# Four graph layers on one core: a new hand-set plan for VectorE's order, and gathers released in batches of four

## The chip, the core and the metric

The kernel runs on one core of one Trainium2 chip. The core has five engines that run side by side, each working off its own list of instructions in order: TensorE (PE, with its weight loads shown as PEld), VectorE (DVE), ScalarE (ACT), GpSimd (POOL) and SyncE (SP, which here only starts transfers). The metric is the time of one execution on the device in microseconds (us), the median of several executions; lower is better.

## What is computed

There are 16 graphs of 1024 nodes with 64 features each and a dense 1024 x 1024 weighted adjacency matrix per graph, of which only a few entries in a row are not zero. Four layers follow each other, each with a layer norm and a ReLU ahead and a residual sum behind:

```python
h = relu(layernorm(x)); x = x + (tanh(concat(h, adj @ h) @ W1 + b1) @ W2 + b2)     # layer 0
h = relu(layernorm(x)); x = x + ((adj + I) @ h) / rowsum(adj + I)                  # layer 1
h = relu(layernorm(x)); x = x + mlp(h + agg(h, dilate(adj)))                       # layer 2
h = relu(layernorm(x)); x = x + ((adj @ h) / colsum(adj)) @ Wn + h @ Ws + bias     # layer 3
```

In layer 2, `dilate` takes some neighbours out of each node's list, and `agg` is a weighted sum of the 0.25, 0.5 and 0.75 quantiles, feature by feature, over the neighbours that are left. That is a sort of a short, ragged list of 64-wide rows for every node, and it is where most of the work lies.

## The kernel before

**Nodes in order of their number of neighbours.** For each graph the kernel ranks the 1024 nodes by their count of remaining neighbours and cuts the ranking into eight blocks of 128 nodes, one node on each of the 128 partitions. A block needs room for as many neighbours as its largest node has; `PLACES = [21, 19, 17, 16, 15, 13, 12, 11]` is how many neighbours of a block are fetched by gathers. `GROUPS` puts the blocks in five groups: block 0 alone (38 places, the longest lists being filled in by packed rows), block 1 alone, and then three pairs of blocks (2,3), (4,5), (6,7), which are sorted two at a time side by side.

**Six streams and a planner.** The work of a graph is cut into six Python generators: `adjacency` (loads the adjacency, transposes it, finds the neighbours to drop, ranks the nodes), `layers` (layers 0 and 1 and the norm of layer 2), `tail` (the rest of layer 2, layer 3 and the output), `gathers`, `neighbour_lists` (finds for each node the indices of its neighbours, eight at a time with MAX8) and `sorts` (the sorting network and the weighted sums). The streams run on different graphs at the same time. The order in which their instructions are put into each engine's list is fixed when the program is built, by a small planner at the end of `direct_path`. It keeps an imagined clock for each engine (`clk.dve`, `clk.pe`, `clk.act`, `clk.pool`). A stream adds its estimated costs to these clocks and then yields the imagined time at which its next result will be there, its due time. The planner takes the first stream, in the order in which they are named above, whose due time is not after `clk.dve`; if there is none, it moves `clk.dve` on to the earliest due time. The helper `after(dve, pe, act, lat)` computes a due time: the work of each engine behind that of the one before, and `lat` on top. Nothing of this clock exists on the chip. There every engine takes its list in order and waits at an instruction whose input is not there yet, with all that stands behind it.

**Gathers and their gate.** A gather is an indirect DMA that GpSimd starts: it fetches one row of 64 features for each of 128 nodes from the table `h_d` in DRAM into the tile `raw` (line 1274, 124 of them in a graph). GpSimd also starts the loads of the key rows that `neighbour_lists` searches (line 1086, eight in a graph, tile `k`), the packed rows (line 1255, three in a graph) and the return gather of the sums, `res` (line 1346, eight in a graph). The gate (lines 912 to 918) ties GpSimd to VectorE: VectorE writes a one-element mark, and GpSimd copies it, so that GpSimd does not go past this point before VectorE has come to the mark in its own list. A gate is set at most once in 4.0 us of the imagined VectorE clock. In `gathers` it is asked for at every fourth place `s`; for a pair of blocks that is every eight gathers.

**Lines that the prediction's steps touch.** 846 to 856 `preln`, the layer norm, with two due times; 940 and 962 the start and the end of the first half of `adjacency`; 998 and 1003 the marks of the dropped neighbours, one for each of eight blocks; 1038 and 1040 two tiles `spread` that VectorE writes and TensorE multiplies with ones, both in one buffer of the tag `ab`; 1045 the eight ACT passes that count for the ranking and 1048 VectorE's `pos` made of them; 1101, 1110 to 1117 the rounds of MAX8, one round of three instructions for each eight neighbours after the first eight; 1192 and 846 the handover from layer 0 to the next norm (`stat<-pt`); 1217 the first VectorE instruction that reads the sums of layer 1 (`den`); 1360 the first that reads the perceptron of layer 2 (`mid`); 1395 the first that reads layer 3; 1307 the compare-exchange steps of the sorting network; 1326 the weighted sums.

Of the kernel before, what the change touches and what calls it, by code (L numbers as in the profile page):

```python
# [11 lines left out]
U16 = mybir.dt.uint16  # L12
# [43 lines left out]
PLACES = [21, 19, 17, 16, 15, 13, 12, 11]  # L56
PACKS, NPACK = [(0, 0, 21, 2, 64), (1, 0, 23, 1, 32), (1, 32, 24, 4, 24), (2, 0, 28, 10, 12)], 3
KB = 4

# [670 lines left out]
def direct_path(ctx: ExitStack, tc: tile.TileContext, t: dict, out: bass.AP, flag):  # L730
# [70 lines left out]
    nc.gpsimd.dma_start(mask8, nodemask.rearrange("b (i p) -> (b i) p", p=P))  # L801
    maskf = lists.tile([B * NB, P], F32, tag="ab", name="maskf", bufs=1)
    nc.vector.tensor_copy(maskf, mask8)
# [37 lines left out]
    def preln(u, x, ha):  # L841

        s = nodes.tile([P, 4, NB], F32, name="stat")
        xc = mid(u, [P, NB, C])
        sq = mid(u, [P, NB, C])
        nc.vector.tensor_reduce(s[:, 0], x, AX.X, ALU.add)
        ts(s[:, 1], s[:, 0], 1.0 / C, None, op0=ALU.mult)
        tt(xc, x, s[:, 1, :, None].to_broadcast([P, NB, C]), ALU.subtract)
        act(sq, xc, AF.Square)
        yield after(1.5, act=0.65)  # L850
        nc.vector.tensor_reduce(s[:, 2], sq, AX.X, ALU.add)
        act(s[:, 3], s[:, 2], AF.Sqrt, bias=eps, scale=1.0 / C)
        yield after(0.7, act=1.0)
        nc.vector.reciprocal(s[:, 2], s[:, 3])
# [57 lines left out]
    def gate():  # L912
        if not marks or clk.dve > marks[-1] + 4.0:
            k = len(marks)
            nc.vector.memset(slots[:, k % 8:k % 8 + 1], 0.0)  # L915
            clk.dve += 0.15
            nc.gpsimd.tensor_copy(opened[:, k % 2:k % 2 + 1], slots[:, k % 8:k % 8 + 1])  # L917
            marks.append(clk.dve)
# [14 lines left out]
    def adjacency(b):  # L933
# [26 lines left out]
        sf = nodes.tile([P, 4, NB], F32, name="sf")  # L960
        yield clk.act + 0.3
        tt(mn[:, 2], mn[:, 0], mn[:, 1], ALU.add)
# [20 lines left out]
        for i in range(NB):  # L983
            following = flipped(i + 1) if i + 1 < NB else None

            p = bank2()
            for j in range(NB):
                o, e = j * P, (j // 4 + 1) * 512
                nc.tensor.matmul(p[:, o:e], nbt[:, j, :], stair[:, :e - o], start=j % 4 == 0, stop=j % 4 == 3)  # L989

            for q in range(2):
                s = slice(q * 512, (q + 1) * 512)
                act(gone[:, i, s], p[:, s], AF.Abs, bias=sf[:, 2 + q, i:i + 1], scale=2.0)  # L993
            nbt = following
            ready = after(0, pe=3.7, act=2.4)
            if waiting:
                yield waiting[1]
                ts(gone[:, waiting[0], :], gone[:, waiting[0], :], sf[:, 1, waiting[0]:waiting[0] + 1], -1.0,
                   op0=ALU.is_equal, op1=ALU.mult)
                clk.dve += 0.5  # L1000
            waiting = (i, ready)
# [34 lines left out]
        for q in range(2):  # L1036
            spread = lists.tile([P, 4, P], F32, tag="ab", name="spread", bufs=1)
            tt(spread, identf[:, None, :].to_broadcast([P, 4, P]),
               key[:, 4 * q:4 * q + 4, None].to_broadcast([P, 4, P]), ALU.mult)
            nc.tensor.matmul(p[:, q * 512:(q + 1) * 512], onesf, spread.rearrange("p j m -> p (j m)"),  # L1040
                             start=True, stop=True)
        over = nodes.tile([P, NB], F32, name="over")
        for i in range(NB):
            sink = lists.tile([P, N], F16, tag="ab", name="sink", bufs=1)
# [9 lines left out]
        nc.vector.tensor_copy(ph, pi)  # L1054
        low = lists.tile([P, NB, P], F16, tag="ab", name="low", bufs=1)
        tt(low, pidx[:, None, :].to_broadcast([P, NB, P]), ph[:, 0, :, None].to_broadcast([P, NB, P]), ALU.is_equal)
# [20 lines left out]
    def neighbour_lists(b):  # L1077
# [5 lines left out]
        def load_keys(i):  # L1083
            if i < NB:
# [12 lines left out]
        for b0, n, cap, *_ in GROUPS:  # L1097
            for i in range(b0, b0 + n):
                src, at = ks[i]
                yield at  # L1100
                nc.vector.max(out=found[:, o:o + 8], in_=src)  # L1101
                clk.dve += 1.15
                yield clk.dve
                less, before = src.bitcast(I16), None
                for r in range(1, -(-cap // 8)):


                    least = found[:, o + 7:o + 8]
                    if r == 1:
                        ts(less, src, least, None, op0=ALU.subtract)  # L1110
                    else:
                        ts(less, less, before, least, op0=ALU.add, op1=ALU.subtract)
                    before = least
                    most = nodes.tile([P, 8], U16, name="most")
                    nc.vector.max(out=most, in_=less.bitcast(U16))  # L1115
                    o += 8
                    ts(found[:, o:o + 8], most.bitcast(I16), 0.0, least, op0=ALU.min, op1=ALU.add)
                    clk.dve += 1.8
                    yield clk.dve
                o += 8  # L1120
                load_keys(i + KB)
        index = lists.tile([P, total], I32, name="index")
# [51 lines left out]
    def layers(b):  # L1174
# [17 lines left out]
        nc.scalar.copy(x, p)  # L1192
        yield after(0, pe=1.3, act=2.1) + 2.8
        ha = nodes.tile([P, NB, C + 1], F32, name="ha")
# [18 lines left out]
        done.add(("adjt", b))  # L1213
        yield after(0, pe=10.5, act=1.1) + 2.5
        clk.act += 10
# [21 lines left out]
    def gathers(b):  # L1237
        g = state[b]
        yield max(g["rows_at"], clk.pool)
        for k, (b0, n, cap, *_) in enumerate(GROUPS):  # L1240
            while not (b == 0 or ("sort", b - 1, k) in done):
                yield None
            raw = raws.tile([P, cap, n * C], F32, name=f"raw{k}")
            o = sum(c * -(-r // 8) * 8 for _, c, r, *_ in GROUPS[:k])
            clk.pool = max(clk.pool, clk.dve)
# [6 lines left out]
            if k == 0:  # L1252
                packed = nodes.tile([P, NPACK * C], F32, name="packed", bufs=1)
                for l, size in enumerate(sizes):
                    nc.gpsimd.indirect_dma_start(packed[:size, l * C:(l + 1) * C], None, h_ds[b % 3],
                                                 bass.IndirectOffsetOnAxis(ap=g["pack"][:size, l:l + 1], axis=0))
                    clk.pool += 1.27
                rows_d = dram.tile([NPACK, P, C], F32, name="rows_d")
            for s in range(cap):
                if s % 4 == 0:  # L1260
                    gate()
# [7 lines left out]
                for i in range(n):  # L1269
                    if s >= PLACES[b0 + i]:  # L1270
                        continue
                    clk.pool += 1.27
                    at = o + i * -(-cap // 8) * 8 + s
                    nc.gpsimd.indirect_dma_start(raw[:, s, i * C:(i + 1) * C], None, h_ds[b % 3],  # L1274
                                                 bass.IndirectOffsetOnAxis(ap=g["index"][:, at:at + 1], axis=0))
                if s % 4 == 3:
                    yield clk.pool - 5
# [62 lines left out]
    def tail(b):  # L1340
# [51 lines left out]
        zn = per_node(bank(), mt, w3n, 4)  # L1392
        yield after(0, pe=2.6)
        o = mid(1, [P, NB, C])
# [16 lines left out]
    programs = [_program(*group[2:]) for group in GROUPS]  # L1411
    edge = lists.tile([1, 2, C], F32, tag="ab", name="edge", bufs=1)
    nc.vector.memset(edge[:, 0], 0.0)
# [165 lines left out]
```

## Time and profile before

| | before |
|---|---|
| median of 3 executions | 4034.94 us (4027.11 to 4052.91) |
| span of the profiled execution | 4035.0 us |
| TensorE busy | 2059.4 us, 51% |
| VectorE busy | 3070.5 us, 76% |
| ScalarE busy | 1426.3 us, 35% |
| GpSimd busy | 2592.2 us, 64% |
| mean granted TensorE clock | 0.676 |

The profile counts an engine as busy while one of its instructions runs. On GpSimd a gather is busy only while its transfer is being set up; the short gap to the next one is listed as idle time that "issue" ended. The views used below are the page itself, the groups of instructions by line (a row has the line, engine and operation, the tiles, the count, the busy time, the mean of one in ns, and the idle time ahead of them with what ended it), the list of waits (who waited, for whom, us in total, times, longest), the timeline (start, length, engine, line, and in brackets the idle time ahead), and the busy time by stage.

### The profile page before, as it was taken

The numbers are of one execution on the slowest core, as the hardware profiler recorded it, in microseconds if no ns is written. First come the engines' busy times: TensorE is split into PE (matmuls) and PEld (weight loads), VectorE is DVE, ScalarE is ACT, GpSimd is POOL, SyncE is SP. The second block draws the span as 40 slices with busy tenths as digits, with TensorE's granted clock in tenths as the row PEclk, the third lists the DMA queues.
The fourth block names the chain that finished last, engine by engine and source line by source line (L and its number), as shares of the span: only waits on it lengthen the run. The fifth ranks groups of instructions, "written<-read, shape, count | busy, mean of one in ns | idle before, by whom it ended". The sixth has DMA issues, their size and how long they took to land.

```text
span 4035.0 us, 32061 instructions
## 1 busy us (share of the span) xinstructions
PE 2059.4 (51%) x8483; PEld 1008.6 (25%) x8483; DVE 3070.5 (76%) x7173; ACT 1426.3 (35%) x2658; POOL 2592.2 (64%) x2608
## 2 busy tenths in 40 slices
PE   7543745446464556456555564544655465544033
PEld 3312322222322223132322223222232222212011
DVE  2647877788687979868776888957969786996973
ACT  6523434333444334244343434323344343331000
POOL 1166666667576768747666676846857666775772
PEclk9665757767666677666667675666667667766555
DMA  2314133232524333242332424323252332323111
GB/s 96 114 40 123 48 115 93 86 107 53 163 50 143 76 107 98 57 134 62 124 84 78 115 65 128 79 76 105 51 164 53 125 88 86 84 62 111 44 47 57
DMA packets 237344, 362.40 MB, mean 90 GB/s; under 512 B 126848, under 2 KB 128496, under 8 KB 237152
## 3 DMA queue, kind: packets, MB, share of 16 engines
q1 hardware_dynamic: 156912, 255.00, 18.4%
q0 software_dynamic: 80096, 104.70, 12.8%
q8 instruction: 69, 1.13, 0.1%
q14 instruction: 123, 1.01, 0.1%
q10 hardware_dynamic: 144, 0.56, 0.0%
HBM read 245.26 MB, written 114.81 MB: 89 GB/s over the span
## 4 chain that ended last, share of the span: by engine, by line
DVE 51%; PE 13%; another core or an unknown queue 12%; issue 10%; ACT 6%; DMA 4%; POOL 4%; DVEq 0%; SPq 0%; ACTq 0%; POOLq 0%
DVE other L1307 14%; DVE raw L1307 14%; PE pt L875 6%; DVE most L1115 4%; POOL raw L1274 4%; DVE agg L1326 2%; DVE found L1101 2%; ACT adjt L1210 2%; PE pt L899 1%; DMA adjt_d<-adjt 1%; DVE nb L940 1%; ACT nb L954 1%; DVE k L1110 1%; DMA raw<-h_d,index 1%
## 5 line engine op out<-in xcount | busy, mean ns | idle before, releaser
L1274 POOL DMA_INDIRECT raw<-h_d,index x1984 | 2164.2, 1091 | 575.4 <-issue 548.5
L875 PE MATMUL pt<-adjt,ha 128*65 128x512 f32 (+1 forms) x1024 | 491.7, 642 | 169.4 <-DVE ha L1197 92.2
L1307 DVE TENSOR_TENSOR other<-raw 128x512 f32<-128x512 f32 (+11 forms) x816 | 536.1, 688 | 43.9 <-DMA raw<-h_d,index 27.3
L917 POOL COPY gate<-mark 1x1 f32<-1x1 f32 x293 | 96.6, 330 | 477.8 <-DVE mark L915 457.6
L947 PE MATMUL pt<-ef,a 128*128 128x128 f32 x1024 | 222.1, 388 | 299.9 <-ACT adjt L948 168.5
L1307 DVE TENSOR_TENSOR raw<-other 128x512 f32<-128x512 f32 (+10 forms) x464 | 356.4, 792 | 6.5 <-DVE other L1307 1.1
L989 PE MATMUL pt<-eh,nbt 128*128 128x512 f16 (+3 forms) x1024 | 207.1, 358 | 225.5 <-ACT nbt L978 152.0
L1115 DVE MAX8 most<-k 128x8 uint16<-128x1024 uint16 x224 | 275.1, 1228 | 15.4 <-DVE k L1110 4.1
L875 PEld LDWEIGHTS pt<-adjt,ha 128*65 128x65 f32 (+1 forms) x1024 | 149.2, 149 | 491.9 <-issue 432.0
L947 PEld LDWEIGHTS pt<-ef,a 128*128 128x128 f32 x1024 | 181.5, 206 | 336.5 <-ACT adjt L948 192.9
L1086 POOL DMA_INDIRECT k<-keys_d,node x128 | 131.4, 1026 | 208.8 <-DVE node L1071 112.9
L1022 ACT ACTIVATE nb<-pt 128x1024 f16<-128x1024 f32 x128 | 130.5, 1020 | 355.1 <-PE pt L1018 113.6
L876 ACT COPY big<-pt 64x1024 f32<-64x1024 f32 (+1 forms) x32 | 32.2, 1007 | 559.6 <-PE pt L875 300.0
L948 ACT COPY adjt<-pt 128x512 f32<-128x512 f32 x256 | 138.9, 583 | 242.1 <-PE pt L947 80.6
L1307 DVE TENSOR_TENSOR raw<-other,raw 128x640 f32<-128x640 f32 (+3 forms) x448 | 216.9, 495 | 7.7 <-remote 1.9
L1307 DVE TENSOR_TENSOR raw<-raw,other 128x128 f32<-128x128 f32 (+7 forms) x496 | 212.4, 437 | 12.2 <-remote 4.4
L1307 DVE TENSOR_TENSOR other<-other,raw 128x128 f32<-128x128 f32 (+4 forms) x448 | 201.8, 461 | 8.2 <-remote 2.3
L954 ACT ACTIVATE nb<-nb 128x512 f16<-128x512 f16 x256 | 159.7, 630 | 135.1 <-DVE nb L942 68.6
L993 ACT ACTIVATE gone<-pt,sf 128x512 f16<-128x512 f32 x256 | 162.8, 691 | 112.2 <-remote 46.5
L1018 PE MATMUL pt<-eh,gone 128*128 128x128 f16 x1024 | 132.7, 261 | 124.5 <-DVE gone L1003 37.8
L989 PEld LDWEIGHTS <-nbt 128*128 128x128 f16 x1024 | 102.9, 114 | 321.0 <-ACT nbt L978 164.3
L978 ACT COPY nbt<-pt 128x1024 f16<-128x1024 f16 x128 | 128.5, 1015 | 146.6 <-remote 106.4
(182 smaller groups left out, 4402.1 us busy)
## 6 DMA issues: line engine op xcount, KB each, us to landing
a<-in_adj_dram SPq DMA_DIRECT2D x64, 1024.0 KB
adjt_d<-adjt SPq DMA_DIRECT2D x64, 1024.0 KB
at<-adjt_d SPq DMA_DIRECT2D x128, 512.0 KB
keys_d<-nb SPq DMA_DIRECT2D x64, 512.0 KB
raw<-h_d,index POOLq DMA_INDIRECT x1984
x<-in_x_dram SPq DMA_DIRECT2D x16, 256.0 KB
h_d<-h SPq DMA_DIRECT2D x16, 256.0 KB
agg_d<-agg SPq DMA_DIRECT2D x16, 256.0 KB
```

The lines of the kernel that those rows point to most:

```text
L875: nc.tensor.matmul(p[p0:p0 + n, s], h[:, j, :n], adjt[:, j, s], start=j == 0, stop=j == NB - 1)
L947: nc.tensor.transpose(p[:, u * P:(u + 1) * P], a[:, j * P:(j + 1) * P], identf)
L948: nc.scalar.copy(adjt[:, 4 * q:4 * q + 4, i * P:(i + 1) * P], p.rearrange("p (u m) -> p u m", m=P))
L954: act(nb[:, i, s], nb[:, i, s], AF.Copy, accum_out=mn[:, q, i:i + 1])
L989: nc.tensor.matmul(p[:, o:e], nbt[:, j, :], stair[:, :e - o], start=j % 4 == 0, stop=j % 4 == 3)
L993: act(gone[:, i, s], p[:, s], AF.Abs, bias=sf[:, 2 + q, i:i + 1], scale=2.0)
L1018: nc.tensor.matmul(p[:, d], gone[:, j, i * P:(i + 1) * P], big_i, start=False, stop=j == 4 * q + 3 and i // 4 != q)
L1022: act(nb[:, i, :], p, AF.Relu)
L1086: nc.gpsimd.indirect_dma_start(k, None, g["keys_d"], bass.IndirectOffsetOnAxis(ap=g["node"][:, i:i + 1], axis=0))
L1115: nc.vector.max(out=most, in_=less.bitcast(U16))
L1274: nc.gpsimd.indirect_dma_start(raw[:, s, i * C:(i + 1) * C], None, h_ds[b % 3], bass.IndirectOffsetOnAxis(ap=g["index"][:, at:at + 1], axi ...
L1307: tt(view(two[to], *((i, vi) if greater else (j, vj)), w), view(two[s], i, vi, w), view(two[u], j, vj, w), ALU.max if greater else ALU.min)
```

## The change

The instructions stay nearly the same; what changes is mainly where the planner puts them.

- Due times are set later: in `preln`, at the end of the first half of `adjacency`, in its two loops, ahead of `key`, `pos` and `node`, after each of the two layers in `layers`, and at four places of `tail`. The planner is to hold VectorE's reading instruction back until the result is there, and to put other work ahead of it. Some TensorE costs in the plan grow for the same reason.
- A gather costs 1.39 us in the plan instead of 1.27.
- The gates: asked for after every four gathers in the pairs too, the least distance of two gates is 3.0 us instead of 4.0, and there is one more ahead of a graph's first key rows.
- The tiles of the tag `ab` get the pool's two buffers instead of one.
- The lengths of the neighbour lists come from a table by block, `LISTS`. Block 3 has 16 places to fetch and now finds 16 neighbours instead of 24, so one round of MAX8 less in each graph.

```diff
+LISTS = [40, 24, 24, 16, 16, 16, 16, 16]
...
-        yield after(1.5, act=0.65)
+        yield after(1.5, act=0.65, lat=1.2)
...
-        yield after(0.7, act=1.0)
+        yield after(0.7, act=1.0, lat=1.5)
...
-        clk.pe = max(clk.pe, clk.dve) + 1.5
+        clk.pe = max(clk.pe, clk.dve) + 2.0 * len(hs)
...
-        if not marks or clk.dve > marks[-1] + 4.0:
+        if not marks or clk.dve > marks[-1] + 3.0:
...
-        yield clk.act + 0.3
+        yield clk.act + 4.0
         tt(mn[:, 2], mn[:, 0], mn[:, 1], ALU.add)
...
-            ready = after(0, pe=3.7, act=2.4)
+            ready = after(0, pe=3.7, act=2.4, lat=3.0)
...
-        yield clk.act + 0.3
+        yield clk.act + 2.0
         key = nodes.tile([P, NB], F32, name="key")
...
-            spread = lists.tile([P, 4, P], F32, tag="ab", name="spread", bufs=1)
+            spread = lists.tile([P, 4, P], F32, tag="ab", name="spread")
...
-        yield after(1.6, pe=1.3, act=10.5)
+        yield after(1.6, pe=1.3, act=10.5, lat=2.0)
...
-        yield after(2.3, pe=1.2, act=0.2) - 0.2
+        yield after(2.3, pe=1.2, act=0.2) + 1.5
...
+        gate()
         for i in range(KB):
             load_keys(i)
-        total = sum(n * -(-cap // 8) * 8 for _, n, cap, *_ in GROUPS)
+        total = sum(LISTS)
...
-                for r in range(1, -(-cap // 8)):
+            for r in range(1, LISTS[i] // 8):
...
-        yield after(0, pe=1.3, act=2.1) + 2.8
+        yield after(0, pe=3.4, act=2.1) + 7.0
...
-        yield after(0, pe=10.5, act=1.1) + 2.5
+        yield after(0, pe=14.0, act=1.1) + 6.0
...
-                    clk.pool += 1.27
+                    clk.pool += 1.39
...
-                if s % 4 == 0:
+                if s % (4 // n) == 0:
                     gate()
...
-                if s % 4 == 3:
+                if (s + 1) % (4 // n) == 0:
                     yield clk.pool - 5
...
-        yield after(0, pe=2.2, act=1.5) + 3.2
+        yield after(0, pe=6.5, act=2.1) + 6.0
         o = mid(1, [P, NB, C])
...
-        yield after(0, pe=3, act=0.6, lat=0.5)
+        yield after(0, pe=3.5, act=0.6, lat=3.0)
...
-        yield after(0, pe=2.6)
+        yield after(0, pe=2.6, lat=5.0)
```

More of the change, by code (lines that the diff above doesn't have):

```diff
@@ L801, in direct_path @@
     nc.gpsimd.dma_start(mask8, nodemask.rearrange("b (i p) -> (b i) p", p=P))
-    maskf = lists.tile([B * NB, P], F32, tag="ab", name="maskf", bufs=1)
+    maskf = lists.tile([B * NB, P], F32, tag="ab", name="maskf")
     nc.vector.tensor_copy(maskf, mask8)
@@ L1043, in adjacency @@
         for i in range(NB):
-            sink = lists.tile([P, N], F16, tag="ab", name="sink", bufs=1)
+            sink = lists.tile([P, N], F16, tag="ab", name="sink")
             act(sink, p, AF.Sign, bias=neg[:, i:i + 1], accum_out=over[:, i:i + 1])
-        yield after(1.6, pe=1.3, act=10.5)
+        yield after(1.6, pe=1.3, act=10.5, lat=2.0)
         pos = nodes.tile([P, NB], I32, name="pos", bufs=5)
@@ L1054, in adjacency @@
         nc.vector.tensor_copy(ph, pi)
-        low = lists.tile([P, NB, P], F16, tag="ab", name="low", bufs=1)
+        low = lists.tile([P, NB, P], F16, tag="ab", name="low")
         tt(low, pidx[:, None, :].to_broadcast([P, NB, P]), ph[:, 0, :, None].to_broadcast([P, NB, P]), ALU.is_equal)
@@ L1096, in neighbour_lists @@
         o = 0
[L1097 to L1102, printed above, removed]
-                yield clk.dve
-                less, before = src.bitcast(I16), None
-                for r in range(1, -(-cap // 8)):
[L1108 to L1121, printed above, removed]
+        for i in range(NB):
+            src, at = ks[i]
+            yield at
+            nc.vector.max(out=found[:, o:o + 8], in_=src)
+            clk.dve += 1.15
+            yield clk.dve
+            less, before = src.bitcast(I16), None
+            for r in range(1, LISTS[i] // 8):
+                least = found[:, o + 7:o + 8]
+                if r == 1:
+                    ts(less, src, least, None, op0=ALU.subtract)
+                else:
+                    ts(less, less, before, least, op0=ALU.add, op1=ALU.subtract)
+                before = least
+                most = nodes.tile([P, 8], U16, name="most")
+                nc.vector.max(out=most, in_=less.bitcast(U16))
+                o += 8
+                ts(found[:, o:o + 8], most.bitcast(I16), 0.0, least, op0=ALU.min, op1=ALU.add)
+                clk.dve += 1.8
+                yield clk.dve
+            o += 8
+            load_keys(i + KB)
         index = lists.tile([P, total], I32, name="index")
@@ L1243, in gathers @@
             raw = raws.tile([P, cap, n * C], F32, name=f"raw{k}")
-            o = sum(c * -(-r // 8) * 8 for _, c, r, *_ in GROUPS[:k])
             clk.pool = max(clk.pool, clk.dve)
@@ L1271, in gathers @@
                         continue
-                    clk.pool += 1.27
-                    at = o + i * -(-cap // 8) * 8 + s
+                    clk.pool += 1.39
+                    at = sum(LISTS[:b0 + i]) + s
                     nc.gpsimd.indirect_dma_start(raw[:, s, i * C:(i + 1) * C], None, h_ds[b % 3],
                                                  bass.IndirectOffsetOnAxis(ap=g["index"][:, at:at + 1], axis=0))
-                if s % 4 == 3:
+                if (s + 1) % (4 // n) == 0:
                     yield clk.pool - 5
@@ L1411, in direct_path @@
     programs = [_program(*group[2:]) for group in GROUPS]
-    edge = lists.tile([1, 2, C], F32, tag="ab", name="edge", bufs=1)
+    edge = lists.tile([1, 2, C], F32, tag="ab", name="edge")
     nc.vector.memset(edge[:, 0], 0.0)
```

## The prediction

> **What bounds the kernel now.** I read the page first (busy shares, slices), then the stages, the waits of VectorE and of GpSimd, the groups of GpSimd, and last the timelines of both around single waits.
>
> ```profile
> DVE  2647877788687979868776888957969786996973
> POOL 1166666667576768747666676846857666775772
> ...
> 500.00:3750.00 3250.00, 1719.03 (x7033) 837.03 (x7031) 2585.08 (x6034) 1186.98 (x2213) 2210.38 (x2217) 0.68 0.33 94
> ...
> L1274 POOL DMA_INDIRECT raw<-h_d,index x1984 | 2164.2, 1091 | 575.4 <-issue 548.5 <-DMA raw<-h_d,index 6.7 <-DVE other L1307 5.8
> L917 POOL COPY gate<-mark 1x1 f32<-1x1 f32 x293 | 96.6, 330 | 477.8 <-DVE mark L915 457.6 <-DVE wts L1167 5.4 <-DVE stat L854 4.6
> ...
> DVE mid L1360 <- PE pt L899: 141.2, 11, 24.1
> DVE stat L846 <- ACT x L1192: 77.5, 3, 30.4
> DVE spread L1038 <- PE pt L1040: 75.4, 11, 15.7
> DVE den L1217 <- PE pt L1204: 71.7, 6, 26.0
> DVE den L1217 <- remote: 66.5, 5, 20.2
> DVE mn L962 <- ACT nb L954: 61.2, 7, 18.4
> DVE gone L998 <- ACT gone L993: 45.0, 15, 13.1
> ...
> 1254.96 0.21 DVE L1217 RECIPROCAL den<-pt 128x8 f32<-128x8 f32 x1 [15.62 <-remote]
> ...
> 1250.79 0.94 POOL L1274 DMA_INDIRECT raw<-h_d,index  x1 [0.30 <-issue]
> 1261.92 0.94 POOL L1086 DMA_INDIRECT k<-keys_d,node  x1 [10.19 <-DVE found L1117]
> 1265.26 0.46 POOL L917 COPY gate<-mark 1x1 f32<-1x1 f32 x1 [2.39 <-DVE mark L915]
> ```
>
> The slices show that from 500 to 3750 us nothing changes: the kernel is in a steady state, graph after graph. The starts of `den` (line 1217) of graphs 2 and 16 in the timeline are 327.8 and 3665.3 us, so a graph takes 3337.5/14 = 238 us. Ahead lies a start-up in which there is little to fill in, behind lies the last graph's chain.
>
> GpSimd's 64% hides how full it is. A gather is 1.091 us plus the gap of 0.29 us that "issue" ended, (2164.2 + 575.4)/1984 = 1.38 us. In a graph: 124 gathers are 171 us, 8 key rows, 8 `res` and 3 packed gathers at about 1.3 us are 25 us, 18.3 gates of 0.33 us are 6 us: 202 us of 238. Adding the waits of GpSimd above 0.6 us in the timeline between 500 and 3750 us gives 465 us, 34 us a graph; 202 + 34 is the period. Nearly all of them are gates (457.6 us in 50 waits).
>
> VectorE's waits in the same stretch come to 594 us, 43 us a graph, and they are few and long. The two lists match one for one. The timeline shows it: VectorE stands at `den` for 15.62 us until 1254.96; GpSimd finishes its eight gathers at 1251.73 and then stands 10.19 us until VectorE has moved on, and 2.39 us more at a gate. Other pairs: `mid` 15.61 us (801.56) and a gate 15.89 us (804.87); `mid` 18.59 (1036.05) and a gate 18.74 (1044.66). So the bound is neither engine alone: **GpSimd is the fuller engine, and it stands when VectorE stands at a result that the plan expected earlier.**
>
> **What the Trainium skill says.** PSUM — Partial Sum Buffer, section Engine vs sequencer instructions: the queues of ScalarE, VectorE and GpSimd are strict FIFO. The trace agrees: nothing passes `den` in those 15.62 us. SBUF — State Buffer, section Who interferes with whom: a VectorE instruction with two SBUF inputs contends with a GpSimd instruction that reads SBUF. Sorting the gathers of the timeline by what VectorE did beside them, those with VectorE idle take 0.945 us (228), those mostly beside line 1307, which has two SBUF inputs, 1.177 us (958): it agrees. No page prices a late result; those prices are from the trace.
>
> **The change part by part.** *Later due times.* These remove no work. They gain when the wait is longer than nothing and other work (sorts, lists) is planned ahead. I take every wait of the timeline between 500 and 3750 us and subtract the added lead, never below zero:
>
> - `den` (1217): lead 3.5 (TensorE 10.5 to 14.0) + 3.5 = 7.0 us. 13 waits, 160.6 us, of 3.8 to 26.0; left 78.
> - `mid` (1360): `paired` 1.5 to 4.0, TensorE 2.2 to 6.5, ACT +0.6, latency +2.8: 10.2 us. 9 waits, 110 us; left 31.
> - `mn` (962): +3.7 us. 7 waits, 70 us; left 45.
> - `stat` of the second norm (846): 2.1 + 4.2 = 6.3 us. 2 waits, 30 us; left 19.
> - `gone` (998): +2.7 us, 45 us; left 18.
>
> The leads in `preln`, `key`, `pos`, `node` and layer 3 answer to waits under 10 us in all in this stretch (line 854: 7.2 us in the whole run), and cost nothing, since sorts stand ready to fill them. The 25.3 us at line 1395 lie in the last graph's tail, where there is nothing to fill in; they stay.
>
> *Two buffers for `ab`.* The second `spread` no longer waits for TensorE to read the first: 95 us in the stretch go to 0. TensorE then starts no later, and `pos` behind it waited only once in the run (9.5 us), so little comes back.
>
> Together 511 us of waits become 191; with 84 us of others, 594 become about 275. Removed: 319 us. GpSimd feels 465/594 = 0.78 of it: **250 us less**.
>
> *A gather at 1.39 us.* It agrees with the measured 1.38. In the plan a graph's GpSimd work becomes 124 x 1.39 + 25 = 197 us, close to VectorE's 195 (238 less its 43 of waits), so the plan itself now has less room. No cost by itself.
>
> *More gates.* Batches of four are 6 + 5 + 9 + 8 + 6 = 34 a graph, one more for the key rows, and a few are merged by the 3.0 us rule: about 33 against 18.3, 235 more in the run. VectorE pays a mark of 59 ns, 14 us, hidden as GpSimd is fuller. GpSimd pays 0.33 + 0.16 us for the copy and its gap, less the 0.30 us gap it replaces: 0.19 us, **45 us in all**. Bounds: 0.04 us (the gate at 1241.69 in the timeline: 0.18 + 0.16 - 0.30) and 0.49 us, so 9 to 115 us. What queues behind a gate is four gathers, then key rows and `res`; `sorts` and `tail` wait for those. In pairs (84 of 124 gathers) a standing VectorE now stops GpSimd up to four gathers (5.5 us) sooner, on the mean 2.7 us. With about 20 long waits left, 20 x 2.7 x 0.68 = **37 us**.
>
> *A denser VectorE.* Of the 228 gathers that ran beside an idle VectorE, half now run beside work: 114 x 0.16 = **18 us** (0.16 is towards 1.10, between the two means above).
>
> *A round of MAX8 less.* 16 x (0.58 + 1.23 + 0.25) = 33 us of VectorE, less the 14 us of marks. It is not the fuller engine; but lists come a little sooner. I take **15 us less**, between 0 and 33.
>
> Sum: 4035 - 250 + 45 + 37 + 18 - 15 = **3870 us**.
>
> **The rivals.** *A: the waits nearly vanish and GpSimd's own work is the bound.* A moved instruction finds all earlier results ready, and one wait less leaves the later ones shorter. Three quarters of the 465 us gone: 4035 - 349 + 45 + 18 = about 3750; all gone would be 3630. For it: 202 us of GpSimd work plus 5 of gates are far below 238. Against: `den` waited up to 26 us, beyond any lead. *B: the waits come back elsewhere.* Where VectorE does not stand at `den`, TensorE has had less time for what follows, and `mid` waits longer; TensorE is held up in its own list by ACT's copies behind the stores of `adjt_d` (ACT line 948 waited 6.99 us for that transfer just ahead of 1255.24), which no due time mends. Then only the `spread` part counts: 4035 - 0.78 x 95 + 45 = about 4005. *C: slower.* The finer tie passes every VectorE wait on in full and the waits stay: (594 - 95) - 465 = +34 us, gates at their upper price +115, denser +18: about 4200, or 4130 with gates at 0.19. For it: GpSimd is the fuller engine and gets more instructions and more waits. Against: single blocks already have batches of four, and waits beside them are no longer than their VectorE waits.
>
> **How the numbers follow.** Forecast (3800 to 3940) 0.50; A (below 3800) 0.20; B (3940 to 4075) 0.19, half of it still more than 1% faster; C (above 4075) 0.11. Faster 0.80, same 0.09, slower 0.11. The range leaves out the lowest twentieth of A and C with the top of B: 3690 to 4030.
>
> **What would show it.** In the changed profile: waits at 1360 and 1217 about a quarter and half of before, none at 1038 for TensorE; waits of gates for marks about half of 457.6 us while the gates are some 530; 208 instead of 224 in line 1115's row; a mean gather above 1.10 us. The period of `den` should be near 228 us. It would be wrong if gates wait more in total than before, if TensorE's results are waited for at other lines as long as before, or if VectorE begins to wait for `raw` or `k`.

## The result and the profile after

| | before | changed |
|---|---|---|
| median of 4 executions | 4043.93 us (4027.11 to 4056.91) | 3902.79 us (3897.33 to 3908.08) |
| ratio, 95% interval | 1 | 0.967 (0.963 to 0.971) |
| `den` of graph 2 to `den` of graph 16 | 3337.5 us, 238.4 a graph | 3180.6 us, 227.2 a graph |
| waits of VectorE in that stretch | 593 us | 457 us |
| waits of GpSimd above 0.6 us in it | 449 us | 323 us |
| gates | 293 | 477 |

The change is 3.3% faster. The numbers by stretch here and below are sums over the timelines of VectorE and GpSimd from the start of the first `den` to that of the second. The page of the changed kernel, and its stretch from 500 to 3750 us (the columns are TensorE, its weight loads, VectorE, ScalarE, GpSimd, the granted clock, the DMA share and GB/s):

```profile
DVE  1557878879687897888787798899699876979482
POOL 1077576776667686776776777777778686777781
500.00:3750.00 3250.00, 1731.58 (x7174) 834.86 (x7172) 2680.18 (x6451) 1183.11 (x2237) 2358.08 (x2475) 0.69 0.34 97
```

It is the same steady state, a little denser: VectorE's busy time in the stretch rises from 2585 to 2680 us and GpSimd's from 2210 to 2358. Some 255 us of this stretch already lie behind the last `den` of the changed kernel. From `den` to `den` the work is the same and the share rises: VectorE is busy for 2643 of 3181 us (83%), where it was busy for 2664 of 3338 us (80%). The groups on GpSimd, and the MAX8 rounds:

```profile
L1275 POOL DMA_INDIRECT raw<-h_d,index x1984 | 2148.8, 1083 | 559.0 <-issue 533.1 <-DVE mark L917 9.2 <-DVE other L1308 4.9
L919 POOL COPY gate<-mark 1x1 f32<-1x1 f32 x477 | 163.9, 344 | 416.2 <-DVE mark L917 369.3 <-DVE den L1219 19.4 <-DVE other L1308 10.2
L1117 DVE MAX8 most<-k 128x8 uint16<-128x1024 uint16 x208 | 255.4, 1228 | 13.2 <-DVE k L1112 3.3 <-remote 2.2 <-DVE k L1114 0.7
```

A gather is no longer than before. The gates wait less, and 124.5 of their 369.3 us are one wait in the start-up: the new gate ahead of the key rows stands where the key rows themselves stood before (112.9 us). The waits of VectorE over the whole run, with the total, the number and the longest:

```profile
DVE other L1308 <- DMA raw<-h_d,index: 113.9, 17, 25.7
DVE stat L853 <- ACT mid L851: 96.3, 14, 16.8
DVE stat L856 <- ACT stat L854: 64.3, 9, 19.0
DVE gone L1000 <- ACT gone L995: 52.5, 10, 15.7
DVE found L1103 <- DMA k<-keys_d,node: 51.2, 11, 14.4
DVE mn L964 <- ACT nb L956: 46.3, 5, 13.6
DVE den L1219 <- remote: 40.7, 5, 15.1
...
DVE mid L1361 <- PE pt L901: 24.4, 2, 24.1
```

The lines that led the list before, `mid`, `spread` and `den`, are further down or gone. At the head stand lines that waited little before: a sort that waits for its gathers (113.9 us, 27.3 before), and the two statistics of the norm that wait for ScalarE (6.6 and 7.2 us before).

What holds the norm up is seen in the timelines of one such wait (start, length, engine, line, and in brackets the idle time ahead and what ended it). TensorE, then ScalarE (seven more passes of line 1212 left out), VectorE, GpSimd:

```profile
980.68 16.80 PE L877 MATMUL pt<-adjt,ha 128*65 128x512 f32 x32 [0.90 <-DVE ha L1199]
997.32 0.60 PE L1204 MATMUL pt<-ha,ef 128*128 128x260 f32 x2
...
1011.83 1.01 ACT L878 COPY big<-pt 65x1024 f32<-65x1024 f32 x1 [23.46 <-remote]
1012.74 1.06 ACT L1212 ACTIVATE adjt<-adjt 128x1024 f32<-128x1024 f32 x1
...
1021.06 0.62 ACT L851 ACTIVATE mid<-mid 128x512 f32<-128x512 f32 x1
...
1021.71 0.69 DVE L853 TENSOR_REDUCE stat<-mid 128x8 f32<-128x512 f32 x1 [16.81 <-ACT mid L851]
1022.32 0.20 DVE L1219 RECIPROCAL den<-pt 128x8 f32<-128x8 f32 x1
...
1022.55 0.18 POOL L919 COPY gate<-mark 1x1 f32<-1x1 f32 x1 [13.81 <-DVE den L1219]
```

`den` itself starts at once. Ahead of it the planner has put the statistic of another stream's norm. Its square (line 851) stands in ScalarE's list behind the copy of layer 1's sums (line 878) and behind the eight passes of line 1212, which belong to `den`'s own stream. So VectorE waits for the same TensorE result as before, handed on by that copy, and for 8.3 us of ScalarE on top. The Trainium skill (PSUM — Partial Sum Buffer, section Engine vs sequencer instructions) says that ScalarE's queue is strict FIFO as well; this trace agrees, for the square of 0.62 us passed none of the nine instructions ahead of it. And GpSimd still stands with VectorE, 13.81 us at its gate. This is the longest wait at line 853 and not the only kind. Of the 14 above 2.5 us in this run (117.5 us), four (40 us) come directly behind line 1212; the squares of the others stand behind passes of `adjacency` in ScalarE's list (lines 1027, 1047 and others), some of which had waited for TensorE themselves.

A second thing is in these lines. TensorE went on to line 1204 at 997.32 us, so line 877 was done by then as far as the profile's modelled ends of matmuls tell, yet the copy that needed it began 14 us later, with no releaser in the trace ("remote"). VectorE stood from 1004.90 us on, so 6.9 of its 16.81 us lie ahead of the copy and belong to this late release; the rest is ScalarE's list. That turned out to matter.

### The profile page after: what moved, and what is told of

Its sections match the earlier page's. It is cut to its first block, busy times and chain, and to the rows that moved or that the text cites. A ratio compares the mean times of both kernels' runs of the same rounds, so it can differ in the third digit from the quotient of the medians.

```text
span 3895.5 us, 32579 instructions
## 1 busy us (share of the span) xinstructions
PE 2044.1 (52%) x8483; PEld 988.9 (25%) x8483; DVE 3035.7 (78%) x7309; ACT 1410.1 (36%) x2658; POOL 2644.1 (68%) x2792
## 4 chain that ended last, share of the span: by engine, by line
DVE 42%; issue 14%; PE 12%; another core or an unknown queue 9%; ACT 8%; POOL 8%; DMA 5%; SPq 0%; DVEq 0%; ACTq 0%; POOLq 0%
DVE other L1308 12%; DVE raw L1308 11%; POOL raw L1275 6%; PE pt L877 5%; DVE most L1117 4%; ACT adjt L1212 2%; DVE found L1103 2%; DVE agg L1327 2%; ACT sink L1047 2%; DMA k<-keys_d,node 1%; DMA raw<-h_d,index 1%; PE pt L901 1%; DVE k L1112 1%; DVE nb L942 1%
## 5 line engine op out<-in xcount | busy, mean ns | idle before, releaser
L1308 DVE TENSOR_TENSOR other<-raw 128x512 f32<-128x512 f32 (+11 forms) x816 | 536.7, 688 | 151.7 <-DMA raw<-h_d,index 113.9
L919 POOL COPY gate<-mark 1x1 f32<-1x1 f32 x477 | 163.9, 344 | 416.2 <-DVE mark L917 369.3
L949 PE MATMUL pt<-ef,a 128*128 128x128 f32 x1024 | 207.5, 360 | 320.8 <-ACT adjt L950 129.6
L1117 DVE MAX8 most<-k 128x8 uint16<-128x1024 uint16 x208 | 255.4, 1228 | 13.2 <-DVE k L1112 3.3
L949 PEld LDWEIGHTS pt<-ef,a 128*128 128x128 f32 x1024 | 157.7, 185 | 408.2 <-issue 180.6
L1384 PE MATMUL tm<-at,ha 128*64 128x512 f32 x512 | 174.1, 785 | 50.0 <-DMA at<-adjt_d 44.4
L1103 DVE MAX8 found<-k 128x8 f32<-128x1024 f16 x128 | 156.3, 1221 | 51.2 <-DMA k<-keys_d,node 51.2
L1347 POOL DMA_INDIRECT res<-agg_d,pos x128 | 135.7, 1060 | 74.9 <-DMA agg_d<-agg 37.4
```

The costliest lines, as they stand in the source:

```text
L949: nc.tensor.transpose(p[:, u * P:(u + 1) * P], a[:, j * P:(j + 1) * P], identf)
L1308: tt(view(two[to], *((i, vi) if greater else (j, vj)), w), view(two[s], i, vi, w), view(two[u], j, vj, w), ALU.max if greater else ALU.min)
L1347: nc.gpsimd.indirect_dma_start(res[:, i, :], None, g["agg_d"], bass.IndirectOffsetOnAxis(ap=g["pos"][:, i:i + 1], axis=0))
L1384: nc.tensor.matmul(p[q * C:(q + 1) * C, :], ha[:, j, :], even(ats[j], q), start=j == 0, stop=j == NB - 1)
```

## The experiments

The kernel before took 3699.89 us in the first set of runs, 3986.22 in the second and 3700.53 in the third, on different chips; so each ratio is to the kernel before in its own set, on the same chip. At least four executions of each new kernel were timed. In these sets the kernel before was profiled in the second only. The expectations of the first set are in us of the first profile, where it took some 4035 us; as the chip was another, only their ratios to that can be held against the results.

| set, before | kernel | us | ratio (95% interval) |
|---|---|---|---|
| 1, 3699.89 | later due times alone | 3873.87 | 1.047 (1.045 to 1.048) |
| | gates alone | 3680.59 | 0.994 (0.993 to 0.996) |
| | 1.39 alone | 3743.01 | 1.012 (1.010 to 1.013) |
| | two `ab` buffers alone | 3646.3 | 0.985 (0.983 to 0.987) |
| 2, 3986.22 | before again | 3980.55 | 0.999 |
| | changed kernel again | 3843.92 | 0.967 (0.962 to 0.971) |
| | changed, no gates | 4477.76 | 1.124 (1.116 to 1.131) |
| | changed, old due times | 3814.39 | 0.958 (0.955 to 0.961) |
| 3, 3700.53 | changed, old gates | 3677.64 | 0.994 (0.992 to 0.996) |
| | changed, old list of block 3 | 3701.59 | 1.000 (0.999 to 1.001) |
| | changed, 1.38 for 1.39 | 3686.41 | 0.996 (0.994 to 0.997) |
| | changed, old due times | 3670.48 | 0.992 (0.990 to 0.993) |

**Later due times alone.** All due times and TensorE costs of the change, put into the kernel before:

```diff
-        yield after(0, pe=10.5, act=1.1) + 2.5
+        yield after(0, pe=14.0, act=1.1) + 6.0
...
-        yield after(0, pe=2.2, act=1.5) + 3.2
+        yield after(0, pe=6.5, act=2.1) + 6.0
```

> The kernel before with the later due times and TensorE costs alone (old gates, gather at 1.27, one buffer for ab, old list lengths). Theory T (the later due times take VectorE off results that are not there, and GpSimd's gates follow): VectorE's waits at lines 1217, 1360 and 962 fall by more than half, gate waits fall by about 100 us, time 3900 to 3970 us. Rival G (the finer gates do it): within 40 us of 4035. Rival P (the gather's cost in the plan does it): within 40 us of 4035.

Measured: 4.7% slower, which none of the three had (0.97 to 0.98, and within 1% of 1). The waits are small where theory T said: `den`, `mid` and the gates wait 23.0, 24.1 and 36.6 us in the whole run, and `mn` is gone. The time rose all the same. Its other waits of VectorE and of GpSimd:

```profile
DVE other L1307 <- DMA raw<-h_d,index: 244.7, 33, 24.9
DVE spread L1038 <- PE pt L1040: 155.2, 16, 19.1
...
POOL packed L1255 <- DMA pack<-pack_d: 217.6, 23, 24.9
```

VectorE waits at `spread`, for TensorE, and for gathers. GpSimd no longer stands at gates but at the packed rows, whose indices have not come back through DRAM (`pack_d`) yet; the gathers behind them in its list are late, and then sorts wait. The largest waits stand at lines whose due times had not been changed.

**Gates alone.**

```diff
-        if not marks or clk.dve > marks[-1] + 4.0:
+        if not marks or clk.dve > marks[-1] + 3.0:
...
+        gate()
         for i in range(KB):
...
-                if s % 4 == 0:
+                if s % (4 // n) == 0:
                     gate()
...
-                if s % 4 == 3:
+                if (s + 1) % (4 // n) == 0:
                     yield clk.pool - 5
```

The last of these edits lets the planner leave `gathers` after every four gathers in the pairs too, so the order changes and not only the number of gates.

> The kernel before with the gate edits alone: batches of four gathers in pairs, least distance 3.0, one gate ahead of the first key rows. Theory T: some 180 more gates at 0.19 us are 35 us, and VectorE's waits stay near 590 us and pass on sooner: 4040 to 4110 us. Rival G: VectorE's and GpSimd's waits both fall, 3900 to 3980 us.

Measured: 0.6% faster, with 469 gates. That is neither the 35 us and more that theory T added nor the gain of rival G. More gates cost nothing here that the time shows.

**1.39 alone, and two buffers alone.** First the planned gather, then the tag `ab`:

```diff
-                    clk.pool += 1.27
+                    clk.pool += 1.39
```

> The kernel before with a gather at 1.39 us in the plan instead of 1.27, and nothing else. Theory T: no wait that VectorE had is mended, 4000 to 4070 us. Rival P: the plan keeps step with GpSimd, gate waits fall by 100 us or more, below 3980 us.

```diff
-            spread = lists.tile([P, 4, P], F32, tag="ab", name="spread", bufs=1)
+            spread = lists.tile([P, 4, P], F32, tag="ab", name="spread")
```

> The kernel before with two buffers for the tag ab and nothing else; the planned order stays what it was. Theory T: the wait at line 1038 goes from 126 us to near 0, and 0.78 of the 95 us in the steady stretch reaches the time: 3960 us; if the time that was waited there comes back at den and mid, 4000 to 4030 us.

Measured: 1.39 alone 1.2% slower, although it is the truer price, where no change or a gain was expected; the buffers alone 1.5% faster (54 us), the largest gain of any single part and close to what was expected (0.981). The waits of VectorE in the kernel with two buffers:

```profile
DVE mid L1360 <- PE pt L899: 142.1, 11, 24.1
DVE found L1101 <- DMA k<-keys_d,node: 91.8, 15, 13.6
DVE den L1217 <- PE pt L1204: 59.8, 14, 13.9
```

`spread`, which waited 75.9 us in the kernel with 1.39 alone and 108.5 in that with the gates alone, is gone from the list. Whether part of its time came back at `found` (91.8 us here) can't be told, since the kernel before has no profile on this chip. `den` waits 14 times, but some 4 us each, with the due times of before, where they took 12 us each in the first profile. The planned order is the same.

**The two kernels again.** Neither has an edit.

> The kernel before, unchanged, profiled beside the experiments, where it took 3700 us and not 4035 us. Theory C (conditions: something outside the plan holds the engines up in the first two profiles, which show waits for a remote or unknown releaser, 798 us before and 575 us after): 3700 us, no such waits, waits at line 1217 a few us each instead of up to 26. Rival: the difference lies in the build, and the profile shows another order of instructions.

> The changed kernel, unchanged, profiled beside the experiments. Theory C: without the remote waits the later due times have less to mend; the later due times alone were 4.7% slower here, so 3700 to 3850 us, slower than before. Rival T (the parts together gain whatever the conditions): below 3660 us, ratio near 0.97.

Measured: the ratio repeats to 0.001 on a chip where both take some 1.5% less. The changed kernel's waits are at the same lines (in the stretch 105 us at line 853, and 65 at line 1308, 30 of them for gathers), so the new waits belong to the plan and not to one execution. Both expectations had counted on the chip of the first set. This was another one, and the profile of the kernel before shows waits with unknown releasers here as in its first profile (701 us), so theory C was not tested by these two runs.

**The changed kernel without gates.**

```diff
-        if not marks or clk.dve > marks[-1] + 3.0:
+        if False and (not marks):
```

With the gates goes the 0.15 us that each adds to the imagined VectorE clock, so the order shifts a little too.

> The changed kernel with no gates at all (no marks, no copies; every order that data asks for stays). Theory T (the gates only pass VectorE's waits on to GpSimd): faster than the changed kernel by the gate waits, 100 us or more. Rival D (the gates keep the transfers in the planned order against each other): slower by 50 us or more, with longer waits of VectorE for key rows and of TensorE for res.

Measured: 12.4% slower than before and 16% slower than the changed kernel of its set; the gain that theory T expected did not come. Its waits:

```profile
DVE stat L853 <- ACT mid L851: 272.2, 16, 44.1
...
POOL k L1088 <- DVE node L1073: 582.9, 13, 126.0
POOL res L1347 <- DMA agg_d<-agg: 224.0, 12, 75.8
```

GpSimd is not freed. It runs ahead in its list and stands at the next key rows until VectorE has their indices. A gather gets cheaper (1037 ns against 1087 in the changed kernel of this set), and VectorE waits more. On this chip the tie is worth more than the waits that it passes on; on the chips without late releases it was not tried. Why VectorE and ScalarE get so much worse without it was not separated further; that gathers issued early move DMA traffic to other moments is a possible cause, not a shown one.

**The changed kernel with the due times of before.** It keeps the gates, 1.39, the buffers and the list table. It ran in the second set and again in the third.

```diff
-        yield after(0, pe=14.0, act=1.1) + 6.0
+        yield after(0, pe=10.5, act=1.1) + 2.5
```

> The changed kernel with the old due times and TensorE costs (the finer gates, 1.39, ab in two buffers and the shorter lists stay). Theory C: about what gates, ab and 1.39 gave singly, 3620 to 3700 us, and not slower than the changed kernel. Rival T: slower than the changed kernel by 100 us or more, with waits at lines 1219 and 1361 back to 10 us and more each.

> The changed kernel with the due times of before, once more, on another occasion: if the later due times really take time back, 0.95 to 0.96 again and below the other three here; if 0.958 was chance of that occasion, 0.965 to 0.975.

Measured: 0.958 and 0.992, in each set faster than the changed kernel (0.967) or its nearest copy (0.996). So the later due times take time back in the kernel that they were part of: 0.8% against the changed kernel itself, 0.4% against its nearest copy. Each difference is no larger than what a small shift of the plan can do (1.39 alone cost 1.2%), but both sets agree in sign with each other and with the due times alone. This is the version that beats both kernels in both sets, though the ratio expected for the third set, 0.95 to 0.96, did not come. As the same program ran on two chips, it also shows what differs between them. Groups, waits and the head of the chain, first in the second set, then in the third:

```profile
L1275 POOL DMA_INDIRECT raw<-h_d,index x1984 | 2168.8, 1093 | 544.8 <-issue 512.2
POOL gate L919 <- DVE mark L917: 355.8, 38, 114.4
ACT big L878 <- remote: 272.5, 11, 34.5
DVE den L1219 <- PE pt L1206: 164.8, 14, 15.0
DVE 47%; issue 13%; another core or an unknown queue 10%; PE 8%; POOL 8%; ACT 7%; DMA 7%; DVEq 0%; SPq 0%; ACTq 0%; POOLq 0%
```

```profile
L1275 POOL DMA_INDIRECT raw<-h_d,index x1984 | 2164.1, 1091 | 540.0 <-issue 478.2
POOL gate L919 <- DVE mark L917: 192.5, 29, 112.7
DVE pos L1050 <- ACT sink L1047: 100.7, 15, 10.5
DVE den L1219 <- PE pt L1206: 80.6, 16, 13.9
DVE 52%; POOL 11%; PE 11%; issue 11%; DMA 10%; ACT 4%; DVEq 0%; POOLq 0%; ACTq 0%; SPq 0%
```

In these two profiles a gather takes as long on both chips, and so does a sort step (688 and 689 ns in line 1308's largest row). TensorE does not: it is busy for 1982.8 us in the second set, at a mean granted clock of 0.695, and for 1918.9 us in the third, at 0.710. These 64 us are less than half of the 144 us between the two times, and TensorE is busy for only 52% of either. The larger difference is waiting: 80 waits with an unknown releaser (606 us over all engines, nearly all on ScalarE) against none, and `den` and the gates wait about twice as long.

The 606 us are the whole idle time ahead of these instructions and not a loss of that size: line 878 stood 572.3 us in all in the second set, and 498.6 us in the third, where every such wait is put down to TensorE. What is late is the release. By the trace's times of the semaphore updates, these 80 came 1.5 to 22 us behind the end of the last instruction that updates the same semaphore, and 78 of these instructions are TensorE's, whose ends are modelled. What part the clock has in it was not tested. As each chip was seen on one occasion, chip and occasion are not told apart either.

**The changed kernel with the old gates, with the old list of block 3, and with 1.38.** In this order:

```diff
-        if not marks or clk.dve > marks[-1] + 3.0:
+        if not marks or clk.dve > marks[-1] + 4.0:
...
-        gate()
         for i in range(KB):
...
-                if s % (4 // n) == 0:
+                if s % 4 == 0:
...
-                if (s + 1) % (4 // n) == 0:
+                if s % 4 == 3:
```

> The changed kernel with the gates of before (every fourth place, 4.0 us, none ahead of the key rows); later due times, two ab buffers, 1.39 and the shorter lists stay. Theory (the finer gates keep GpSimd in the planned order and are a main part of the gain; the later due times alone cost time): slower than the changed kernel by 2 to 5%, so a ratio to before of 0.98 to 1.02, with about 290 gates and waits of VectorE for raw above 150 us. Rival of the record (gates only cost, +45 and +37 us): faster than the changed kernel by about 2%, ratio near 0.945.

```diff
-LISTS = [40, 24, 24, 16, 16, 16, 16, 16]
+LISTS = [40, 24, 24, 24, 16, 16, 16, 16]
```

> The changed kernel with 24 instead of 16 places in the list of block 3, so with the sixteen rounds of MAX8 back; nothing else is changed. Prediction's step (15 us, between 0 and 33): ratio to before 0.966 to 0.975. Rival (VectorE's work counts more than taken, since the plan shifts with it): above 0.98.

```diff
-                    clk.pool += 1.39
+                    clk.pool += 1.38
```

> The changed kernel with a gather at 1.38 us in the plan instead of 1.39, a change without any meaning on the chip: it measures how much the time moves when only the places of instructions shift a little. If the plan's small shifts do nothing: 0.967, as the changed kernel. If they count: anything from 0.95 to 0.985, and then differences of 1% between single edits say little on the edit itself.

Measured: 0.994, 1.000 and 0.996. The changed kernel itself did not run in this set. Its copy with 1.38 stands for it, and is only 0.4% faster than before; all four of its near copies here lie between 0.992 and 1.000. So the 3.3% is not what the change is worth everywhere, as far as these copies tell. It also means that the copy with 1.38 could not measure what it was made for, how much a shifted price moves the time. With the old gates it is no slower (my expectation, 2 to 5% slower, was wrong: a tie was needed where it was taken out, but not the finer one here), and its gate waits fall from 174.2 us in the copy with 1.38 to 57.5, since the 125 us of the start-up are at the key rows again, while those for the packed rows' indices grow from 67.6 to 96.7. Against the copy with 1.38, the round of MAX8 is worth 15 us, as predicted; the two kernels differ in the price as well. As it takes a step of 0.4% for a whole part of the change, and a price shifted by 0.12 us costs 1.2%, single differences of this size say as much about the placing as about the edit.

The wait at the norm is in this set too. TensorE, ScalarE and VectorE in the copy with 1.38:

```profile
1367.74 16.36 PE L877 MATMUL pt<-adjt,ha 128*65 128x512 f32 x32 [6.97 <-DVE ha L1199]
...
1384.14 1.01 ACT L878 COPY big<-pt 65x1024 f32<-65x1024 f32 x1 [20.66 <-PE pt L877]
...
1393.37 0.61 ACT L851 ACTIVATE mid<-mid 128x512 f32<-128x512 f32 x1
...
1394.02 0.69 DVE L853 TENSOR_REDUCE stat<-mid 128x8 f32<-128x512 f32 x1 [10.26 <-ACT mid L851]
1394.63 0.20 DVE L1219 RECIPROCAL den<-pt 128x8 f32<-128x8 f32 x1
```

Here the copy starts 0.04 us after TensorE's last matmul of line 877, and the square still stands behind it and the eight passes. Of the 13 waits above 2.5 us at line 853 in this kernel (99 us), eight (67 us) come directly behind line 1212. With the due times of before, on the same chip, one wait above 2.5 us is left at line 853, of 4.8 us. But the waits are exchanged more than removed: in the stretch, line 853 goes from 82 to 15 us and line 1308 from 83 to 27, while `pos` goes from 17 to 90, `den` from 0 to 64 and `mid` from 0 to 22; in all VectorE waits 245 us in place of 259. The program text says why the plan did not see the eight passes: `clk.act += 10`, the price of those eight passes, stands behind `den`'s `yield`, while the passes themselves are put into ScalarE's list ahead of it. Whatever the planner places between, and a later due time makes that more, is planned on a ScalarE that looks free. Whether the right place for this line would bring the norm's waits down was not tried.

## Why the prediction was right and wrong

The time and the direction were right: 3870 us was predicted and 3902.79 measured, within the range, and the gain is 141 us of the 165 predicted. The period of 227.2 us a graph was predicted too (near 228). The reason given for it was wrong in its main step, and that the sum still came near is luck, since two errors cancel. GpSimd's waits fell by 127 us from `den` to `den`, where the prediction takes off 213 (250, with 37 given back by the gates): 86 us too few. The rest of GpSimd's time fell by 30 us, where the prediction adds 48 (45 for gates, 18 for a denser VectorE, 15 off for MAX8): 78 us too many.

- **What bounds the kernel**: right. GpSimd's work of 202 us a graph is still there (204, the period less its waits), and its longest wait in the example above still mirrors VectorE's (13.81 and 16.81 us).
- **Later due times, 250 us less with the buffers**: the step that failed. At their own lines the waits fell by what I took, or more:

| line, us in the stretch | before | predicted | measured |
|---|---|---|---|
| `den` | 160.6 | 78 | 36.9 |
| `mid` | 105 | 31 | 3.5 |
| `mn` | 69.9 | 45 | 46.3 |
| `stat`, second norm | 42.1 | 19 | 14.8 |
| `gone` | 38.6 | 18 | 5.8 |
| `spread` | 95.1 | 0 | 0 |
| all others | 82 | 84 | 350 |

  (The predicted values were taken from the stretch from 500 to 3750 us, so a line's value before differs a little. The 45 us that the prediction takes for `gone` are those of the whole run; the stretch has 36.6, which would make the 250 us about 6 us smaller.) The term that was mis-sized is the last row, which I left as it was. Of the 350 us, 165 are at lines 853 and 856, where I had written that the later due times of `preln` "cost nothing, since sorts stand ready to fill them", 57 are at the sort steps of line 1308 (39 of them for gathers), 48 for key rows. VectorE's waits fell by 136 us and not 319. The runs put the balance of the due times on the other side: alone they cost 4.7%, and the changed kernel is 0.8% faster without them on the same chip.
- **GpSimd feels 0.78 of it**: it lost 127 us of waits, 0.93 of VectorE's 136.
- **More gates, 45 and 37 us**: too high. There are 477, some 50 fewer than the 530 predicted; the period without GpSimd's waits went from 206 to 204 us, and the gates alone made the kernel 0.6% faster. My view that a tie only passes waits on missed what it does: without any, the kernel is 12% slower than before, on the chip where that was tried. But the finer tie as against the coarse one is not shown to gain inside the changed kernel.
- **A denser VectorE, 18 us**: wrong in sign; the mean gather is 1.083 us and not above 1.10. The gathers beside an idle VectorE did not become fewer (some 10% in the stretch both times), and a smaller share ran mostly beside line 1308 (46%, 49% before).
- **The MAX8 round, 15 us**: right in size; the list with it put back costs 0.4%, 15 us, though that is also the size of the plan's chance shifts.
- **Two buffers**: right in the wait, `spread` went to 0; alone they gained 54 us on another chip, where 74 were taken from 95 us of waits. Whether little came back elsewhere, as I took it, is not shown.
- **The rest of the balance**: the stretch from `den` to `den` gained 157 us, the start-up 14 us, and the end lost 31 us (370 to 401 us behind the last `den`); the sum is the 140 us between the two profiled spans. No step spoke of the end.
- **The rivals**: B's mechanism, waits that come back elsewhere, is what the due times did, and the sign I gave for it came true: VectorE began to wait for `raw` and `k` (51.2 us at the key rows, 10.1 before). Its time did not come; which other parts made up for it is open. A stayed away: 323 us of GpSimd's waits are left. So did C.
- **What no step held**: that a part of the waits of before was not the plan's. Where the kernel before takes some 3980 us or more, part of its wait at `den` lies behind late releases; the row "den <- remote, 66.5" in the list of waits before was such a sign, and I added it to the plan's errors. Even the wait that the prediction shows, `den` at 1254.96 us, is one. TensorE's last matmul for it stands in the first profile as

```profile
1241.42 1.00 PE L1204 MATMUL pt<-ef,big 65*128 65x65 f32 x8
```

  which ends at 1242.42 us, so 12.5 of the 15.62 us came behind it. Over all waits at `den` it is 62 of the 160.6 us, by the modelled ends. The waits at `mid` have none of it. Where no release is late, the kernel before takes 3700 us, and the near copies of the changed kernel are left with 0 to 0.8%.

Open: why the releases come late on some chips; which of the buffers, the gates, the price of 1.39 and the list table gives the 4.2% there that the changed kernel has with the due times of before, since the parts were run alone only where there are none; and why 1.39 alone costs time. The whole is not the sum of the parts: the four ratios of the first set multiply to 1.037, while the copy of the changed kernel gives 0.996. The two buffers in the kernel before, at 0.985, were the best of all where no release is late.

## What to carry to other kernels

Here a planner that orders one engine moved waits, as it did not count all that it had already put into the other engines' lists. Before raising a due time, look at what will stand on ScalarE and TensorE ahead of the work that is pulled forward. So an estimate of what a later due time gains has to name the work that will wait in its place. Add up the waits after a change over all lines and not at the lines that were mended, and put each part of a change alone into the kernel before, on one chip. A wait whose releaser the trace doesn't know is not evidence for a mistake in the plan: compare when the producer's last instruction ended.

## What was not expected of the hardware

- The same program took 3814 us on one chip and 3670 on another, with equal durations of gathers and sort steps and 64 us more of TensorE. In the slower run 80 waits ended at an update that came 1.5 to 22 us late, 78 of them at one of TensorE's; in the faster run there is none. In the example above ScalarE's copy began 14 us after the matmuls that it needed.
- Waits with an unknown releaser grow when GpSimd is untied: 1442 us in the changed kernel without gates, 655 in the changed kernel of the same set. What links the two was not found.
- A gather beside an idle VectorE took 0.95 us, and 1.17 us mostly beside line 1308, in the changed kernel; 0.95 and 1.18 us in the one before.
